# Attention in six TensorE runs a group, and the third gate ahead of the first down, in a perceiver layer

## The chip, the cores and the metric

The kernel runs on one core of one Trainium2 chip. The metric is device time in microseconds of one execution, the median of three runs. Five engines take part: TensorE (PE in the profile; PEld is its weight load), VectorE (DVE), ScalarE (ACT), GpSimd (POOL) and SyncE (SP), which here only issues DMAs. Each engine takes its instructions in the order in which they were emitted.

## The reference

One layer with three stages, all in float32: 16 sequences of 64 tokens of width 1024 attend to a context of 1601 rows each; a gated FFN of inner width 2752 keeps, in each row, only the half of the gate's values that are largest in magnitude; eight rank-16 experts with a top-2 router are added. Cut to what matters:

```python
x = x + xattn(layernorm(x), ctx, ctx, mask)      # 32 heads of 32, 8 KV heads
scores = einsum('bsgrd,btgd->bgrst', xq, xk) / sqrt(32) + mask
probs = softmax(scores)
out = einsum('bgrst,btgd->bsgrd', probs, xv)

s = silu(layernorm(x) @ w_gate.T)
s[the k = 1376 smallest |s| of each row] = 0
x = x + (s * (h @ w_up.T)) @ w_down.T

x = x + experts(layernorm(x))                    # top 2 of 8, rank 16
```

## The kernel before, in words

**Attention.** The work is cut into 64 groups (`Group`, L235): a sequence, one half of the KV heads (4 heads), and half of the query repeats, so that a group has 4 heads with 128 query rows each and 1601 context columns. A group passes through these steps:

- `scores(c)`: for part c of the columns (`PARTS`, L29: 289, 512, 288 and 512 columns), four products, one for each head, each on 32 of TensorE's 128 rows. They go to four PSUM banks: heads 0 to 2 to a bank of their own each (`ps_s`), head 3 to the shared pool `ps_t`.
- `masked(c)`: DVE adds the mask, writes the scores to `sc` in SBUF and takes the maximum over the part; after the last part one small reduction (`nm`) makes the maximum of the row.
- `softmax(g)`: ACT takes the exponential of head g in place, 1601 columns, with its sum.
- `turn(heads)`: TensorE transposes the two heads' 13 blocks of 128 columns. They fill seven tiles of `ps_t`: three of four blocks for each head and one for both last blocks of 65 columns. The tiles are copied to `pT` in SBUF, the first five by ACT, the rest by DVE (one wide copy and two narrow ones).
- `values(c0, c1)`: for blocks c0 to c1, the product of pT with v, each head on 32 of TensorE's columns, summed in the one bank of `ps_o`.
- `keep()`: ACT copies the output of the group to `oT`, DVE takes the reciprocals of the sums.

PSUM has eight banks: `ps_s` three, `ps_o` one, and `ps_t` four (L145). A pool hands its banks out in rotation: the fifth tile gets the bank of the first, and its writer waits until that was read. `ps_t` also holds the query transposes (`turn_queries`) and the transposed outputs (`finish_tile`).

The order is written out by hand in the loop over groups n (L418), in two halves d. In half d TensorE does the long part (512 columns) of the next group's scores, the transposes of heads 2d and 2d+1 of group n, a short part of the scores of group n+1 (d = 0) or n+2 (d = 1), and half of the values of group n-1. That makes eight runs of TensorE in a group. Query transposes of the next tile of tokens stand in the second half of two groups in eight. While attention runs, POOL makes sums and differences of the weights' quarters for the FFN and writes them back to DRAM.

**FFN.** Gate (g), up (u) and down (d) products use seven products of half-size blocks in place of eight, for pairs of token tiles; there are four pairs. Between g and d of a pair, `drop_small` finds each row's threshold: 31 steps, each with one pass of DVE over one tile and one of ACT over the other, then two passes of ranks (`ranks`) to settle ties, and POOL sets the small values to zero. Then TensorE transposes the gated rows (`ptd`), ACT copies them, and the down product follows; then the experts of the pair.

This part is not written out in order. A planner (`Plan`, L1287) simulates the engines when the kernel is built: each step is a task with an engine, an estimated time, its dependencies, a rank and the buffers that it takes, and of the tasks that are ready on an engine, the one with the lowest rank is emitted next. The ranks of the products come from the list `order` (L1235). A task may have a margin: it counts as ready only so long after its dependencies' ends. `normed(..., 15.0)` gives one of 15 us to the normalisation of a pair that is loaded from DRAM.

Of the kernel before, what the change touches and what calls it, by code (L numbers as in the profile page):

```python
# [9 lines left out]
F32 = mybir.dt.float32  # L10
# [10 lines left out]
P = 128  # L21
# [4 lines left out]
NTC = (T + P - 1) // P  # L26
TL = T - (NTC - 1) * P

PARTS = [(0, 289), (289, 801), (801, 1089), (1089, T)]  # L29
NCH = len(PARTS)  # L30
I = 2752
IC = 344
# [22 lines left out]
def tile_perceiver_layer(  # L55
# [78 lines left out]
    a1 = new_pool(early, "a1", 1)  # L134
    ktp = new_pool(early, "kT", 3)
    qtp = new_pool(early, "qT", 2)
    scp = new_pool(early, "sc", 2)
    xnp = new_pool(late, "xn", 1, "right")
    vp = new_pool(late, "v", 3, "right")
    ptp = new_pool(late, "pT", 8, "right")  # L140
    otp = new_pool(late, "oT", 2, "right")
    twp = new_pool(early, "tw", 3)
    xp = new_pool(late, "x", 3, "right")
# [91 lines left out]
    class Group:  # L235


        def __init__(self, b, h, rh):
            self.b, self.h, self.rh = b, h, rh
            self.name = f"{b}_{h}_{rh}"  # L240
            self.sc, self.pT = {}, {}

        def scores(self, c, spare=False):


            b, h, rh = self.b, self.h, self.rh
            if c == 0:
                self.sc = [
                    scp.tile([P, T], F32, tag=f"sc{g}", name=f"sc{g}_{self.name}")
                    for g in range(4)  # L250
                ]
# [4 lines left out]
            t0, t1 = PARTS[c]  # L256
            homes = [[(ps_s, f"ps{g}"), (ps_t, "pt")] for g in range(3)]
            homes.append([(ps_t, "pt"), (ps_o, "po")])
            self.ps = []
            for g in range(4):  # L260
                home, tag = homes[g][spare]
                ps = home.tile([P, 512], F32, tag=tag, name=f"ps{g}_{self.name}_{c}")
                self.ps.append(ps)
            for g in range(4):
                rows = slice(g * HD, (g + 1) * HD)
                q = qT[b // 2][rows, h, b % 2, 2 * rh : 2 * rh + 2, :]
                pe.matmul(
                    self.ps[g][:, : t1 - t0],
                    q.rearrange("p r s -> p (r s)"),
                    kv[b][0][h][rows, t0:t1],  # L270
                    start=True,
                    stop=True,
                )

        def masked(self, c, heads=range(4)):


            t0, t1 = PARTS[c]
            for g in heads:
                dve.tensor_tensor_reduce(  # L280
                    out=self.sc[g][:, t0:t1],
                    in0=self.ps[g][:, : t1 - t0],
                    in1=mask2[:, t0:t1],
                    scale=1.0,
                    scalar=LOWEST,
                    op0=ALU.add,
                    op1=ALU.max,
                    accum_out=self.mx[:, g, c : c + 1],
                )
            if c == NCH - 1 and 2 in heads:  # L290
                self.nm = small.tile([P, 4], F32, tag="nm", name=f"nm_{self.name}")
                dve.tensor_reduce(self.nm, self.mx, AX.X, ALU.max, negate=True)

        def softmax(self, g):

# [108 lines left out]
        pe.transpose(warm[:, 0, :], ident, ident)  # L404
    for h in range(2):
        turn_queries(0, xn, h)
    for group, c in [(groups[0], c) for c in range(NCH)] + [(groups[1], c) for c in range(2)]:
        group.scores(c, spare=c % 2 == 1)
        if c % 2 == 0:
            for _ in range(4):  # L410
                pe.transpose(group.ps[3][:, 3 * P :], ident, ident)
        group.masked(c)
    for g in range(2):
        groups[0].softmax(g)

# [2 lines left out]
    for n in range(ng):  # L418
        i, m = n // 8 + 1, n % 8
        group = groups[n]  # L420
        last = n == ng - 1
        if m == 2 and i < NT:
            load_x(i)
        if m == 4 and n > 8:
            sp_queue.dma_start(xs[i - 2], x[i - 2])
        if n == ng - 3:
            for j in range(2):
                x[j] = xp.tile([P, D], F32, tag="x", name=f"x{j}_f")
                sp_queue.dma_start(x[j], xs[j])
        for d in range(2):  # L430
            add = None
            long = (groups[n + 1], 2 * d + 1) if n + 1 < ng and n + d > 0 else None
            short = (groups[n + 1 + d], 2 - 2 * d) if n + 1 + d < ng else None
            if long:
                long[0].scores(long[1])
            if i < NT and d == 1 and m >= 6:
                turn_queries(i, xn, m - 6)
            if n > 8 and 3 <= 2 * m + d <= 4:
                copy, add = finish_tile(i - 2, 1 - d)
                act.copy(*copy)  # L440
            copies = group.turn((2 * d, 2 * d + 1))
            on_act = 3 if last else 5
            for copy in copies[:on_act]:
                act.copy(*copy)
            if long:
                long[0].masked(long[1], (3, 0, 1, 2))
            for copy in copies[on_act:]:
                dve.tensor_copy(*copy)
            if short:
                short[0].scores(short[1])  # L450
                short[0].masked(short[1])
            if d == 0:
                for g in (2, 3):
                    group.softmax(g)
            elif n + 1 < ng:
                for g in range(2):
                    groups[n + 1].softmax(g)
            if add:
                add()
            if n > 0:  # L460
                groups[n - 1].values(*((0, NTC // 2), (NTC // 2, NTC))[d])
                if d == 1:
                    groups[n - 1].keep()
            if i < NT:
                if (m, d) == (4, 0):
                    norm = Norm(x[i], f"q{i}")
                if (m, d) in ((4, 0), (5, 0)):
                    norm.half(m - 4)
                if (m, d) == (5, 1):
                    norm.end()  # L470
                    xn = scaled_rows(i, norm, pool)
            if d == 1 and 0 <= n - 3 < 3 * NU:
                sums_made(n - 3)
                sums_out(n - 3)
            if d == 1 and 0 <= n - 2 < 3 * NU:
                sums_in(n - 2)
            if last:
                xn = first[d].tile([P, D], F32, tag=("xn", "oT")[d], name=f"xn_f{d}")
                norm = Norm(x[d], f"f{d}")
                norm.half(0)  # L480
                norm.half(1)
                norm.end()
                dve.tensor_scalar(xn, x[d], norm.mean, norm.rstd, ALU.subtract, ALU.mult)
                first_xn[d] = xn
# [232 lines left out]
    def gate(pair, n, rank, after):  # L717
# [10 lines left out]
        for i in pair:  # L728

            def start(i=i):  # L730
                s[i] = sp[i % 6 > 1].tile([P, NIB * P], F32, tag="s", name=f"s{i}")
                pool.memset(s[i][:, I:], 0.0)
                if i not in first_xn:
                    nc.sync.dma_start(s[i][:, D : 2 * D], xs[i])

            t = add("POOL", 0.1, start, after(i), rank)
            if i not in first_xn:
                t = normed(
                    lambda i=i: s[i][:, D : 2 * D], lambda i=i: s[i][:, :D], ahead,
                    f"f{i}", [t], 15.0,  # L740
                )
# [25 lines left out]
    def drop_small(pair, n, gated, after, up):  # L767
# [26 lines left out]
            box["cand"] = cand  # L794
            box["over"] = small.tile([P, 2], F32, tag="over", name=f"over{n}")

        t = add("DVE", 3.4, magnitudes, gated[pair[0]] + gated[pair[1]] + after, 1)
        upped = up([t])
        for bit in range(30, -1, -1):

# [64 lines left out]
        for j, i in enumerate(pair):  # L865
# [32 lines left out]

            t = [t] + [ts1] * j + marked[j]
            for h in range(2):  # L900
                t = [add("DVE", 4.1, lambda h=h, f=ranks: f(h), t, 2)]
            t = add("DVE", 0.6, limits, t + [tb[j]], 2)
            for h in range(2):
                t = add("DVE", 1.75, lambda h=h, f=keep: f(h), [t], 2)
# [327 lines left out]
        return done  # L1232

    pairs = [(i, i + 1) for i in range(0, NT, 2)]
    order = ["g0", "u0", "g1", "d0", "u1", "g2", "g3", "d1", "u2", "d2", "u3", "d3"]  # L1235
    rank = {name: 10 + 10 * j for j, name in enumerate(order)}
    gated = [gate(pairs[0], 0, rank["g0"], lambda i: [])]

# [177 lines left out]
```

## Time and profile before

| what | us |
|---|---|
| three runs | 1723.62, 1723.66, 1723.87 |
| median | 1723.66 |
| the profiled execution | 1721.6 |
| its span, first to last instruction | 1719.8 |

Mean granted TensorE clock: 0.997. By stretches of the span (busy us of each engine):

| stretch, us | PE | DVE | ACT | POOL | DMA share |
|---|---|---|---|---|---|
| 0 to 20: loads, first scores | 16.0 | 12.8 | 3.8 | 7.4 | 0.92 |
| 20 to 836: attention | 814.2 | 687.5 | 757.7 | 310.6 | 0.49 |
| 836 to 1720: FFN, experts | 862.1 | 710.9 | 499.3 | 240.7 | 0.85 |

A row of the timeline has the start in us, the time until the end of the last of its instructions, the engine, the line (L93 is the helper that records every instruction), the operation, the tile written and the tile read, their shapes and how many instructions were merged. In brackets stands idle time of the engine before the row and what ended it. The tiles: `ps` scores, `pt` transposes of the softmax, `po` values, `pg_g` and `pg_u` gate and up, `ptd` transposes before the down, `pd` the down. The ends of matmuls are modelled, so one row can reach into the next; the starts are measured. A float32 matmul leaves two load and two matmul records, a transpose one of each.

### The profile page before, as it was taken

The page shows a single profiled execution, that of the slowest core. Times are in us where ns is not written, and L with a number is a line of the kernel's source. Part 1 is how long each engine was busy: PE and PEld are TensorE (multiplying, and loading weights), DVE is VectorE, ACT ScalarE, POOL GpSimd, SP SyncE. Part 2 cuts the span into 40 slices and gives each one's busy share as a digit, 9 for nine tenths or more (in the row PEclk, how much of TensorE's full clock was granted, in tenths as well). Part 3 has the DMA queues.
Part 4 walks back from the last instruction along what each step waited for, and adds up shares of the span by engine and source line. Part 5 has one row for each costly group of instructions (what it writes and reads, how often), then busy time and mean ns, then how long its engine had stood idle before and what let it go on. Part 6 is the DMA issues. An engine that isn't in the chain of part 4 may idle for free. (4 is left out here: it accounts for less than half of the span.)

```text
span 1719.8 us, 38753 instructions
## 1 busy us (share of the span) xinstructions
PE 1692.3 (98%) x15102; PEld 1151.8 (67%) x15102; DVE 1411.2 (82%) x3655; ACT 1260.8 (73%) x1780; POOL 558.6 (32%) x584
## 2 busy tenths in 40 slices
PE   8999999999999999999999999899999999999999
PEld 6777777777777777777766666446666546645644
DVE  7888888888888888888627999999989999999603
ACT  6999999999999999999544676676737874777010
POOL 2044453454544454110120221512250313332631
PEclk9999999999999999999999999999999999999999
DMA  8236456545556646211599999688989888888873
GB/s 248 85 112 221 144 194 213 186 170 191 172 173 212 204 159 203 70 61 58 193 333 326 307 291 311 210 297 308 301 278 305 266 300 269 285 291 275 317 265 141
DMA packets 132326, 384.56 MB, mean 224 GB/s; under 512 B 9488, under 2 KB 61232, under 8 KB 132144
## 3 DMA queue, kind: packets, MB, share of 16 engines
q1 hardware_dynamic: 113280, 312.83, 55.3%
q0 software_dynamic: 18432, 68.16, 11.7%
q8 instruction: 120, 1.97, 0.5%
q10 hardware_dynamic: 432, 1.09, 0.2%
q14 instruction: 62, 0.51, 0.1%
HBM read 339.58 MB, written 42.47 MB: 222 GB/s over the span
## 5 line engine op out<-in xcount | busy, mean ns | idle before, releaser
L93 DVE CUSTOM_DVE_ANT_0 sc<-ps,mask 128x512 f32<-128x512 f32 (+2 forms) x1024 | 526.3, 571 | 103.1 <-PE ps L93 102.7
L93 ACT ACTIVATE sign<-a,cand 128x2752 int8<-128x2752 f32 x136 | 351.9, 2588 | 107.8 <-DVE cand L93 107.3
L93 ACT ACTIVATE sc<-sc,nm 128x1601 f32<-128x1601 f32 x256 | 420.1, 1666 | 9.6 <-DVE nm L93 9.6
L93 PEld LDWEIGHTS pt<-ident,sc 128*128 128x128 f32 (+1 forms) x3328 | 361.9, 141 | 77.5 <-issue 72.8
L93 PE MATMUL pt<-ident,sc 128*128 128x128 f32 (+1 forms) x3328 | 391.1, 274 | 1.2 <-ACT sc L93 1.1
L93 DVE TENSOR_SCALAR_CACHE_REDUCE junk<-a,cand 128x2752 uint8<-128x2752 f32 x124 | 381.6, 3077 | 3.8
L93 ACT COPY pT<-pt 128x512 f32<-128x512 f32 x636 | 323.8, 607 | 46.2 <-PE pt L93 45.9
L93 PE MATMUL pg_g<-w_g,hS 128*128 128x344 f32 x896 | 263.9, 455 | 6.4 <-DVE s L93 3.3
L93 PE MATMUL pg_u<-w_u,hS 128*128 128x344 f32 x896 | 263.7, 452 | 0.0
L93 POOL TENSOR_TENSOR tw<-tw 128x344 f32<-128x344 f32 (+1 forms) x192 | 176.1, 928 | 267.0 <-DMA tw<-in_wd_dram 89.0
L93 PE MATMUL ps<-kT,qt 32*128 32x512 f32 (+2 forms) x2048 | 247.7, 549 | 3.1 <-DVE mx L93 2.8
L93 PEld LDWEIGHTS pg_g<-w_g,hS 128*128 128x128 f32 x896 | 170.0, 191 | 94.4 <-issue 4.2
L93 PE MATMUL pd<-w_d,s 128*128 128x512 f32 x528 | 231.0, 592 | 0.0
L93 PEld LDWEIGHTS pg_u<-w_u,hS 128*128 128x128 f32 x896 | 168.8, 190 | 86.8 <-issue 3.1
L93 PE MATMUL po<-pT,v 128*32 128x128 f32 x6656 | 208.1, 274 | 0.4 <-ACT oT L93 0.4
L93 PEld LDWEIGHTS po<-pT,v 128*32 128x32 f32 x6656 | 174.1, 110 | 48.6 <-issue 43.7
L93 PEld LDWEIGHTS pd<-w_d,s 128*128 128x128 f32 x528 | 98.6, 190 | 115.3 <-issue 114.8
L93 DVE COPY pT<-pt 65x128 f32<-65x128 f32 (+1 forms) x388 | 141.0, 418 | 23.0 <-PE pt L93 16.0
L93 PEld LDWEIGHTS ps<-kT,qt 32*128 32x128 f32 x2048 | 83.1, 183 | 52.2 <-DVE mx L93 34.8
L93 ACT ACTIVATE s<-s 128x344 f32<-128x344 f32 (+1 forms) x70 | 36.7, 537 | 91.3 <-DVE s L93 90.9
L93 POOL TENSOR_TENSOR s<-s,rank 128x688 f32<-128x688 f32 x32 | 62.4, 1967 | 88.2 <-DVE rank L93 87.4
L93 DVE DVE_READ_ACCUMULATOR2_ANT mx<- 128x1 f32 x1024 | 83.9, 82 | 0.0
(322 smaller groups left out, 1216.5 us busy)
## 6 DMA issues: line engine op xcount, KB each, us to landing
w_g<-ts SPq DMA_DIRECT2D x64, 688.0 KB
w_u<-ts SPq DMA_DIRECT2D x64, 688.0 KB
w_d<-ts SPq DMA_DIRECT2D x48, 768.0 KB
w_g<-in_wg_dram SPq DMA_DIRECT2D x48, 688.0 KB
w_u<-in_wu_dram SPq DMA_DIRECT2D x48, 688.0 KB
w_d<-in_wd_dram SPq DMA_DIRECT2D x36, 768.0 KB
kT<-in_ctx_t_dram SPq DMA_DIRECT2D x31, 800.5 KB
v<-in_ctx_v_dram SPq DMA_DIRECT2D x32, 768.0 KB
```

The lines of the kernel that those rows point to most:

```text
L93: return tc.keep_in_program_order(getattr(self.engine, op)(*args, **kwargs))
```

## The change

**In attention**

- The parts are 512, 512, 512 and 65 columns. The last part is called the rest. Its four products no longer stand in a run with the others: `rests(heads)` makes them for two heads at a time, each into a tile of `ps_t`.
- In half d = 0 of group n, TensorE does part 1 of group n+1, the transposes of heads 0 and 1, the rests of heads 0 and 1 of group n+1 with its part 2, and all values of group n-1. In half d = 1 it does the rests of heads 2 and 3 of group n+1 with part 0 of group n+2, and the transposes of heads 2 and 3. These are six runs.
- The maximum is made for heads 0, 1 and for heads 2, 3 apart (`maxima`). The exponentials of group n+1's heads 0 and 1 are the last of ACT in half 0 and in half 1.
- In half 1 ACT copies four tiles of transposes, DVE two wide and two narrow ones.
- `keep` of group n-1 stands in half 0, ahead of the exponential of head 0. The query transposes stand at the head of half 0.
- Score buffers: two for heads 0, 1, three for heads 2, 3; pT has six buffers for eight. At the start the filler transposes between the scores are gone, and only part 0 of group 1 is made ahead.

**In the FFN's planner**

- The third gate ranks ahead of the first down.
- The margin of a normalisation is 30 for 15; the estimates of `magnitudes` are 4.4 for 3.4 and of `ranks` 4.0 and 5.5 for 4.1.

```diff
-PARTS = [(0, 289), (289, 801), (801, 1089), (1089, T)]
+PARTS = [(0, 512), (512, 1024), (1024, 1536), (1536, T)]
...
-    scp = new_pool(early, "sc", 2)
+    scp = [new_pool(early, "sc", 2), new_pool(early, "sc_late", 3)]
...
-    ptp = new_pool(late, "pT", 8, "right")
+    ptp = new_pool(late, "pT", 6, "right")
...
+        def rests(self, heads):
+            for g in heads:
+                self.rest[g] = ps_t.tile(
+                    [P, 512], F32, tag="pt", name=f"rest{g}_{self.name}"
+                )
+                self.product(g, NCH - 1, self.rest[g])
...
+        def maxima(self, j):
+            if j == 0:
+                self.nm = small.tile([P, 4], F32, tag="nm", name=f"nm_{self.name}")
+            heads = slice(2 * j, 2 * j + 2)
+            dve.tensor_reduce(
+                self.nm[:, heads], self.mx[:, heads], AX.X, ALU.max, negate=True
+            )
...
+        after = groups[n + 1 : n + 3] + [None, None]
         for d in range(2):
             add = None
-            long = (groups[n + 1], 2 * d + 1) if n + 1 < ng and n + d > 0 else None
-            short = (groups[n + 1 + d], 2 - 2 * d) if n + 1 + d < ng else None
-            if long:
-                long[0].scores(long[1])
-            if i < NT and d == 1 and m >= 6:
+            if i < NT and d == 0 and m >= 6:
                 turn_queries(i, xn, m - 6)
+            ahead, c = (after[0], 1) if d == 0 else (after[1], 0)
+            if d == 1 and after[0]:
+                after[0].rests((2, 3))
+            if ahead:
+                ahead.scores(c)
...
             copies = group.turn((2 * d, 2 * d + 1))
-            on_act = 3 if last else 5
+            on_act = 3 if last else 5 - d
             for copy in copies[:on_act]:
                 act.copy(*copy)
-            if long:
-                long[0].masked(long[1], (3, 0, 1, 2))
+            if d == 1 and after[0]:
+                after[0].masked(NCH - 1, (2, 3))
+            if ahead:
+                ahead.masked(c)
+            if d == 1 and after[0]:
+                after[0].maxima(1)
             for copy in copies[on_act:]:
                 dve.tensor_copy(*copy)
-            if short:
-                short[0].scores(short[1])
-                short[0].masked(short[1])
             if d == 0:
                 for g in (2, 3):
                     group.softmax(g)
-            elif n + 1 < ng:
-                for g in range(2):
-                    groups[n + 1].softmax(g)
+                if after[0]:
+                    after[0].rests((0, 1))
+                    after[0].scores(2)
+                    after[0].masked(NCH - 1, (0, 1))
+                    after[0].masked(2, (0, 1))
+                    after[0].maxima(0)
+                    after[0].masked(2, (3, 2))
+                if n > 0:
+                    groups[n - 1].values(0, NTC)
+                    groups[n - 1].keep()
+            if after[0]:
+                after[0].softmax(d)
             if add:
                 add()
-            if n > 0:
-                groups[n - 1].values(*((0, NTC // 2), (NTC // 2, NTC))[d])
-                if d == 1:
-                    groups[n - 1].keep()
...
-                    f"f{i}", [t], 15.0,
+                    f"f{i}", [t], 30.0,
...
-        t = add("DVE", 3.4, magnitudes, gated[pair[0]] + gated[pair[1]] + after, 1)
+        t = add("DVE", 4.4, magnitudes, gated[pair[0]] + gated[pair[1]] + after, 1)
...
-                t = [add("DVE", 4.1, lambda h=h, f=ranks: f(h), t, 2)]
+                t = [add("DVE", 5.5 if j else 4.0, lambda h=h, f=ranks: f(h), t, 2)]
...
-    order = ["g0", "u0", "g1", "d0", "u1", "g2", "g3", "d1", "u2", "d2", "u3", "d3"]
+    order = ["g0", "u0", "g1", "g2", "d0", "u1", "g3", "d1", "u2", "d2", "u3", "d3"]
```

More of the change, by code (lines that the diff above doesn't have):

```diff
@@ L240, in __init__, with product @@
             self.name = f"{b}_{h}_{rh}"
-            self.sc, self.pT = {}, {}
+            self.sc, self.pT, self.rest = {}, {}, {}
+        def rests(self, heads):
[4 more added lines that the diff above has]
+                self.product(g, NCH - 1, self.rest[g])
+        def product(self, g, c, out):
+            b, h, rh = self.b, self.h, self.rh
+            t0, t1 = PARTS[c]
+            rows = slice(g * HD, (g + 1) * HD)
+            q = qT[b // 2][rows, h, b % 2, 2 * rh : 2 * rh + 2, :]
+            pe.matmul(
+                out[:, : t1 - t0],
+                q.rearrange("p r s -> p (r s)"),
+                kv[b][0][h][rows, t0:t1],
+                start=True,
+                stop=True,
+            )
         def scores(self, c, spare=False):
@@ L248, in scores @@
                 self.sc = [
-                    scp.tile([P, T], F32, tag=f"sc{g}", name=f"sc{g}_{self.name}")
+                    scp[g // 2].tile([P, T], F32, tag=f"sc{g}", name=f"sc{g}_{self.name}")
                     for g in range(4)
@@ L255, in scores @@
                     load_kv(b + 1)
-            t0, t1 = PARTS[c]
             homes = [[(ps_s, f"ps{g}"), (ps_t, "pt")] for g in range(3)]
@@ L264, in scores, with masked @@
             for g in range(4):
[L265 to L275, printed above, removed]
+                self.product(g, c, self.ps[g])
+        def masked(self, c, heads=(3, 0, 1, 2)):
             t0, t1 = PARTS[c]
             for g in heads:
+                ps = self.rest[g] if c == NCH - 1 else self.ps[g]
                 dve.tensor_tensor_reduce(
                     out=self.sc[g][:, t0:t1],
-                    in0=self.ps[g][:, : t1 - t0],
+                    in0=ps[:, : t1 - t0],
                     in1=mask2[:, t0:t1],
@@ L289, in masked @@
                 )
-            if c == NCH - 1 and 2 in heads:
+        def maxima(self, j):
+            if j == 0:
                 self.nm = small.tile([P, 4], F32, tag="nm", name=f"nm_{self.name}")
-                dve.tensor_reduce(self.nm, self.mx, AX.X, ALU.max, negate=True)
+            heads = slice(2 * j, 2 * j + 2)
+            dve.tensor_reduce(
+                self.nm[:, heads], self.mx[:, heads], AX.X, ALU.max, negate=True
+            )
         def softmax(self, g):
@@ L406, in tile_perceiver_layer @@
         turn_queries(0, xn, h)
[L407 to L411, printed above, removed]
+    for j, (group, c) in enumerate(
+        [(groups[0], c) for c in range(NCH - 1)] + [(groups[1], 0)]
+    ):
+        if j == 2:
+            group.rests((0, 1))
+        group.scores(c, spare=j % 2 == 1)
+        if j == 2:
+            group.rests((2, 3))
         group.masked(c)
+        if j == 2:
+            group.masked(NCH - 1, range(4))
+            for half in range(2):
+                group.maxima(half)
     for g in range(2):
@@ L466, in tile_perceiver_layer @@
                     norm = Norm(x[i], f"q{i}")
-                if (m, d) in ((4, 0), (5, 0)):
-                    norm.half(m - 4)
-                if (m, d) == (5, 1):
+                if m == 4:
+                    norm.half(d)
+                if (m, d) == (4, 1):
                     norm.end()
+                if (m, d) == (5, 0):
                     xn = scaled_rows(i, norm, pool)
```

## The prediction

> **What bounds the kernel now.** I read the page first. Its engine rows and slices show a TensorE that is never idle for a tenth of a slice, at full clock:
>
> ```profile
> PE 1692.3 (98%) x15102; PEld 1151.8 (67%) x15102; DVE 1411.2 (82%) x3655; ACT 1260.8 (73%) x1780; POOL 558.6 (32%) x584
> ...
> PE   8999999999999999999999999899999999999999
> ...
> PEclk9999999999999999999999999999999999999999
> ```
>
> A busy PE is not yet a bound PE, since its ends are modelled. So I took the timeline of TensorE alone over one group of the attention (starts count, not ends):
>
> ```profile
> 427.51 0.77 PE L93 MATMUL ps<-kT,qt 32*128 32x289 f32 x8
> 428.21 1.74 PE L93 MATMUL po<-pT,v 128*32 128x128 f32 x56
> 429.88 1.14 PE L93 MATMUL ps<-kT,qt 32*128 32x512 f32 x8
> 430.95 3.06 PE L93 MATMUL pt<-ident,sc 128*128 128x128 f32 x26
> 433.94 0.77 PE L93 MATMUL ps<-kT,qt 32*128 32x288 f32 x8
> 434.63 1.52 PE L93 MATMUL po<-pT,v 128*32 128x128 f32 x48
> 436.08 1.14 PE L93 MATMUL ps<-kT,qt 32*128 32x512 f32 x8
> 437.15 3.06 PE L93 MATMUL pt<-ident,sc 128*128 128x128 f32 x26
> 440.14 0.77 PE L93 MATMUL ps<-kT,qt 32*128 32x289 f32 x8
> ```
>
> From start to start: 0.70, 1.67, 1.07, 2.99, 0.69, 1.45, 1.07, 2.99 us, together 12.63 (427.51 to 440.14). Equal runs take equal times, and the waits of TensorE between 100 and 800 us name no engine for more than 0.4 us at a time: the eight runs stand back to back. ACT idles 0.95 us of such a group (0.51 + 0.44, both waiting for transposes). So PE sets the period, and a cost on PE is a cost of the kernel. Fixed costs come from pairs of runs: scores take (1.07 - 0.70)/223 columns = 1.66 ns a column plus 0.22 us a run; values 0.22 us per 8 records plus 0.13 a run.
>
> Next the two other engines beside the transposes that start at 430.95:
>
> ```profile
> 431.70 2.54 ACT L93 COPY pT<-pt 128x512 f32<-128x512 f32 x5 [0.51 <-PE pt L93]
> ```
> ```profile
> 433.83 1.08 DVE L93 COPY pT<-pt 128x512 f32<-128x512 f32 x3
> ```
>
> ACT copies tiles one to five out of PSUM: the first starts 0.75 us after the run's start, the fifth ends at 434.24, 3.29 after it. DVE starts on the sixth at 2.88, as soon as it is there; the groups of instructions by shape give this DVE copy 0.691 us. The run itself lasts 2.99. **The last tiles of a run are copied after the run ends**; today nobody needs their banks then.
>
> In the FFN TensorE is packed too; its timeline has two places with waits, the start of the first down and the fourth gate:
>
> ```profile
> 1079.64 2.74 PE L93 MATMUL pd<-w_d,s 128*128 128x512 f32 x6
> 1084.28 0.93 PE L93 MATMUL ptd<-ident,s 128*128 128x128 f32 x6 [1.90 <-ACT s L93]
> ...
> 1092.74 0.88 PE L93 MATMUL ptd<-ident,s 128*128 128x128 f32 x6 [0.45 <-POOL s L93]
> ...
> 1099.94 1.54 PE L93 MATMUL ptd<-ident,s 128*128 128x128 f32 x6 [2.99 <-ACT s L93]
> ```
> ```profile
> 1258.07 4.32 PE L93 MATMUL pg_g<-w_g,hS 128*128 128x344 f32 x14 [3.26 <-DVE s L93]
> ```
>
> **The change on TensorE, run by run.** A group becomes six runs: scores part 1; transposes of heads 0, 1; two rests (65 columns) with scores part 2; all values; two rests with the next group's part 0; transposes of heads 2, 3.
>
> Removed: one run of scores and one of values, 0.22 + 0.13 = 0.35 us of fixed cost, and 65 columns of the wide runs, 0.11 us: 0.46 a group.
>
> Added: four rest products in two pairs. By columns alone a pair costs 65 x 1.66 ns = 0.11 us. Here a rule speaks against the change. The Trainium skill (TensorE: Matmul & The Clock Gate, LDWEIGHTS) says a weight load costs its columns over 1.2 GHz, whatever the contraction: 128 columns, an estimated 0.107 us. The trace has two loads to a product (2048 load records for the 1024 score products). Under 512 columns the second load hides; under 65 (0.054 us a pass) it doesn't, so a pair costs 2 x 0.107 = 0.21. No row of before has such a narrow product. Bounds: 0.11 by columns, 0.43 if the two row groups don't overlap at all; eight loads in 0.31 us in the trace say that they overlap. I take 0.21.
>
> Without new waits a group would take 12.63 - 0.46 + 0.42 = 12.59: the gain is nearly eaten by the rests, 2 us over 62 groups; with the rests at 0.11 a pair it would be 12.39, and 15 us.
>
> **The new wait.** Transposes, rests and head 3's scores share a pool of four PSUM banks, in rotation. Today seven transposed tiles are followed by one such tile (head 3 of the short part), which gets the bank of tile four, copied 2.73 us into the run (0.75 + 3 x 0.48 + 0.55): no wait. After the change three follow the first run of transposes: rest 0 gets the bank of tile four, rest 1 that of tile five (ACT, 3.29), head 3 of part 2 that of tile six (DVE, 2.88 + 0.69 = 3.57). PE would be there at 2.99. It issues in order, so head 3 starts at 3.57 + 0.05 (a release by DVE at 25.02 was followed by PE at 25.07) = 3.62, 0.63 late, and then the whole 1.07 of a scores run follows. The rests fit inside that wait, so their 0.21 isn't charged here. Run three takes 0.63 + 1.07 = 1.70.
>
> Sum of a group: 1.07 + 2.99 + 1.70 + 2.99 (1.45 + 1.67 - 0.13) + 1.28 (1.07 + 0.21) + 2.99 = **13.02, against 12.63: +0.39**. For 62 groups (the first and last aside) +24 us.
>
> Behind the waiting PE stand all values of the group before; behind those on ACT the oT copy, and behind that, in ACT's order, the exponential of the next group's head 0. It ends at 8.75 + 0.15 + 0.20 + 1.62 = 10.72 after the group's start; the first tile of the second transposes is there at 8.75 + 1.28 + 0.75 = 10.78. That just fits, so I charge nothing; if it is late, ACT's copies are.
>
> Query turns move to the head of a group (14 groups). The extra tile shifts the rotation: head 3 of part 1 then gets the bank of tile five, which DVE now copies, after its four masks and the maxima: 1.29 + 4 x 0.61 + 0.28 + 0.69 = 4.70 after the scores before, where PE is at 1.07 + 2.99 + 0.44 = 4.50. With 0.05: +0.25, x14 = +3 us.
>
> **DVE, ACT and the rest of attention.** Masks stay 16 a group over the same 1601 columns: 12 x 0.61 + 4 x 0.15 equals 8 x 0.61 + 8 x 0.38 within 0.1. DVE gains one copy (0.6) and one maximum (0.28): from 10.7 to 11.6 of 13.0, still covered, but its masks come closer to tile six: up to 0.1 later, which would go onto the wait. ACT loses a copy (0.48); with PE as the bound that is worth nothing. Pools of SBUF (three late score buffers, six pT for eight): the values that free pT now stand earlier on PE than the copies that need it, so nothing. SP's loads and POOL's weight sums keep their places. Start: sixteen filler transposes go and DVE does the same masks; 0, within 1 us.
>
> **FFN.** With the third gate ahead of the first down, the down's transposes and zeroing (POOL 9.8 us for the first tile) are finished behind 66 us of gate work: the waits 1.90 + 0.45 + 2.99 = 5.3 us go. Total products, weights and DMA are the same, and DVE's selection has slack: it ends near 1560, with 155 us of PE work behind it. What is late next is the fourth gate, which needs the first pair's experts, 66 us later now; u1 and d1 stand ready to fill. The 3.26 us wait comes from DVE's ranks (4.19 us scans) ahead of PSUM sums; the longer planner times should place them better, but the ranks now fall under u1's sums: I take half, 1.6. FFN: -7, bounds -10 (both go, and the 1.4 us holes before expert turns) and +2.
>
> **Sum.** 24 + 3 - 7 = +20. On the profiled execution, 1721.6 us (span 1719.8): 1741.6; the median stands 2.1 above it, 1723.66, so **1743.7 us**.
>
> **Rivals.**
> A, the forecast, 0.66: 1734 to 1754.
> B, the other side, 0.15: the wait for tiles five and six is not there (the pool gives another bank, or the copies end inside the run), and rests cost 0.11 a pair: 12.63 - 0.46 + 0.22 = 12.39, -15 us, and FFN -7: 1702. For it: two switches really go. Against: four banks and 2.88 + 0.69 leave no room. It decides where tile six is free by 2.99; the break-even with FFN's 7 us is a group at +0.11, a wait below about 0.3.
> C, 0.13: a second engine follows. DVE's masks make tile six late and ACT's exponential, queued behind the oT copy, delays the next transposes: 0.1 + 0.2 more a group, +19: about 1762.
> D, 0.06: rests under the scores are free (-0.21) and FFN gains 10: +11 + 3 - 10 = about 1728.
>
> **How the numbers follow.** Two tenths of a per cent, 3.4 us, is about what a measurement of this kernel can tell from no change. B is faster (0.15), D's low end and gaps between cases give same 0.04, the rest slower 0.81. The range 1718 to 1762 holds A and D, half of C, and leaves B out.
>
> **What would show it.** In the changed kernel's TensorE timeline: six runs a group; the run of 65- and 512-column scores after transposes of heads 0, 1 starting with a wait on ACT pT and DVE pT of 0.3 to 0.7 us; 13.0 us between groups; 2.99 us for the 104 value records; the first down without its 5.3 us. Wrong would be: groups of 12.4 to 12.6 with no wait at the rests (B), idle ACT gone (C), or the FFN not shorter.

## The result, and the profile after

| | us |
|---|---|
| before, median of 4 runs beside the change | 1723.64 (1723.26 to 1723.87) |
| after, median of 4 runs | 1755.6 (1751.79 to 1756.05) |
| ratio, with its 95% interval | 1.0184 (1.0172 to 1.0197) |
| predicted | 1743.7, range 1718 to 1762 |
| the profiled execution of after, and its span | 1755.33 and 1753.5 |

The change costs 32 us. The page of after shows as full a TensorE as before, with 30 us more of "busy" time for fewer instructions:

```profile
PE 1722.0 (98%) x15090; PEld 1186.3 (68%) x15090; DVE 1460.6 (83%) x3782; ACT 1237.2 (71%) x1717; POOL 559.1 (32%) x584
...
PE   8999999999999999999999999999989999999999
...
PEclk8999999999999999999999999999999999999999
```

Short waits are covered by the modelled ends of the matmuls and count as busy, so the page can't tell where the time went. The starts can. TensorE's timeline of after over a plain group (one without query transposes), where the brackets with idle time are absent although TensorE waits:

```profile
451.77 3.06 PE L93 MATMUL pt<-ident,sc 128*128 128x128 f32 x26
454.75 0.68 PE L93 MATMUL rest<-kT,qt 32*128 32x65 f32 x3
455.12 0.70 PE L93 MATMUL ps<-kT,qt 32*128 32x512 f32 x2
455.27 0.27 PE L93 MATMUL rest<-kT,qt 32*128 32x65 f32 x1
455.38 1.13 PE L93 MATMUL ps<-kT,qt 32*128 32x512 f32 x6
456.44 3.05 PE L93 MATMUL po<-pT,v 128*32 128x128 f32 x104
459.42 0.33 PE L93 MATMUL rest<-kT,qt 32*128 32x65 f32 x2
459.43 0.70 PE L93 MATMUL ps<-kT,qt 32*128 32x512 f32 x2
459.58 0.28 PE L93 MATMUL rest<-kT,qt 32*128 32x65 f32 x2
459.69 1.08 PE L93 MATMUL ps<-kT,qt 32*128 32x512 f32 x6
460.70 3.06 PE L93 MATMUL pt<-ident,sc 128*128 128x128 f32 x26
463.69 1.14 PE L93 MATMUL ps<-kT,qt 32*128 32x512 f32 x8
464.76 1.42 PE L93 MATMUL pt<-ident,sc 128*128 128x128 f32 x11
```

From start to start: 2.98, 1.69 (rests and part 2), 2.98, 1.28 (rests and part 0), 2.99, 1.07; a group takes 12.99 us (451.77 to 464.76). Two runs with products of the same shapes differ by 0.41 us: the one at 459.42 is free, the one at 454.75 waits. In the free run the last six wide records start 0.27 after the first rest, in the other 0.63 after it. The timelines of ACT and then DVE at the same moment show for what:

```profile
452.51 2.54 ACT L93 COPY pT<-pt 128x512 f32<-128x512 f32 x5 [0.39 <-PE pt L93]
```
```profile
454.64 1.08 DVE L93 COPY pT<-pt 128x512 f32<-128x512 f32 x3
```

ACT's fifth copy ends at 455.05, and then rest 1 can start in the bank of tile five (the third rest record stands at 455.11). The first of DVE's three copies lasts 0.69 us and reads tile six. It ends at 455.33, and at 455.38 TensorE writes head 3's scores into that bank. Tile six is the wait that ends last.

By stretches of the two profiled executions (starts of the first transposes of a group; 33.7 us in all):

| stretch | before | after | difference |
|---|---|---|---|
| start of the span to group 2 | 45.73 | 51.95 | +6.2 |
| group 2 to group 63 (61 groups) | 781.60 | 810.35 | +28.8 |
| group 63 to the first gate product | 18.03 | 17.26 | -0.8 |
| first gate to the last product | 870.1 | 869.5 | -0.6 |

So the attention's groups lose nearly all of it, the start some, and the FFN gives next to nothing back in this execution.

### The profile page after: what moved, and what is told of

Read it like the earlier page. It is cut to its first block, busy times and chain, and to the rows that moved or that the text cites. A ratio compares the mean times of both kernels' runs of the same rounds, so it can differ in the third digit from the quotient of the medians.

```text
span 1753.5 us, 38510 instructions
## 1 busy us (share of the span) xinstructions
PE 1722.0 (98%) x15090; PEld 1186.3 (68%) x15090; DVE 1460.6 (83%) x3782; ACT 1237.2 (71%) x1717; POOL 559.1 (32%) x584
## 4 chain that ended last, share of the span: by engine, by line
PE 72%; DVE 18%; issue 4%; POOL 2%; ACT 2%; DMA 1%; SPq 0%; DVEq 0%; ACTq 0%; POOLq 0%
PE pt L93 20%; PE ps L93 11%; PE po L93 11%; PE pg_u L93 10%; DVE junk L93 10%; PE pd L93 9%; PE pg_g L93 5%; PE rest L93 3%; POOL s L93 2%; DVE sc L93 1%; DVE s L93 1%; DVE rank L93 1%; ACT sign L93 1%; DVE pT L93 1%; DVE cand L93 1%
## 5 line engine op out<-in xcount | busy, mean ns | idle before, releaser
L93 DVE CUSTOM_DVE_ANT_0 sc<-ps,mask 128x512 f32<-128x512 f32 x768 | 488.8, 687 | 65.2 <-PE ps L93 62.3
L93 ACT ACTIVATE sc<-sc,nm 128x1601 f32<-128x1601 f32 x256 | 421.2, 1657 | 11.3 <-DVE nm L93 11.3
L93 PE MATMUL pt<-ident,sc 128*128 128x128 f32 (+1 forms) x3328 | 395.4, 276 | 3.9 <-DVE mx L93 3.5
L93 ACT COPY pT<-pt 128x512 f32<-128x512 f32 x573 | 293.8, 605 | 31.5 <-PE pt L93 31.1
L93 PE MATMUL ps<-kT,qt 32*128 32x512 f32 x1536 | 254.0, 642 | 1.9 <-DVE mx L93 1.7
L93 PEld LDWEIGHTS po<-pT,v 128*32 128x32 f32 x6656 | 177.9, 110 | 47.4 <-issue 47.4
L93 PE MATMUL po<-pT,v 128*32 128x128 f32 x6656 | 195.1, 274 | 0.0
L93 DVE COPY pT<-pt 65x128 f32<-65x128 f32 (+1 forms) x451 | 178.1, 453 | 17.0 <-PE pt L93 10.8
L93 PEld LDWEIGHTS ps<-kT,qt 32*128 32x128 f32 x1536 | 92.4, 186 | 15.1 <-issue 9.1
```

Source lines behind the costliest of these rows:

```text
L93: return tc.keep_in_program_order(getattr(self.engine, op)(*args, **kwargs))
```

## The experiments

### Which half of the change carries the loss

`attn_only` is after with the FFN's planner as before, `ffn_only` is before with the FFN's four edits:

```diff
-                    f"f{i}", [t], 15.0,
+                    f"f{i}", [t], 30.0,
...
-        t = add("DVE", 3.4, magnitudes, gated[pair[0]] + gated[pair[1]] + after, 1)
+        t = add("DVE", 4.4, magnitudes, gated[pair[0]] + gated[pair[1]] + after, 1)
...
-                t = [add("DVE", 4.1, lambda h=h, f=ranks: f(h), t, 2)]
+                t = [add("DVE", 5.5 if j else 4.0, lambda h=h, f=ranks: f(h), t, 2)]
...
-    order = ["g0", "u0", "g1", "d0", "u1", "g2", "g3", "d1", "u2", "d2", "u3", "d3"]
+    order = ["g0", "u0", "g1", "g2", "d0", "u1", "g3", "d1", "u2", "d2", "u3", "d3"]
```

> The changed kernel with the FFN's planner as before. Theory: all of the loss is attention's, 34 us up to the first gate: 1755.6 + 0.6 = about 1756 us, first gate at 879.6 us of the span as in the changed kernel. Rival: the FFN's edits are worth 7 us beside this attention: about 1762 us.

> The kernel before with the four edits of the FFN's planner alone. Theory: in the changed kernel the FFN took 869.5 us from the first gate to the last matmul against 870.1 before, because the waits that go at the first down (5.3 us) and in the fourth gate (3.3 us) come back at the start of the second down, where TensorE has no gate left to fill with. That has nothing to do with attention, so this kernel takes 1723.6 - 0.6 = about 1723 us, with waits of 5 to 10 us between the second up and the second down. Rival (the term of the prediction): the FFN gains 7 us by itself and lost them to something that attention brought: about 1717 us, without those waits.

`attn_only` took 1754.27 us (ratio 1.0178, 1.0157 to 1.0200): within its interval the whole loss. `ffn_only` took 1721.19 (ratio 0.9986, 0.9978 to 0.9994): 2.6 us gained, between the theory (0.6) and its rival (7). The waits at the second down that after shows (below) are in `ffn_only` too, 2.62 and 2.13 us, so the attention doesn't cause them.

### The wait for the banks

`no_first_rests` makes no rest products of heads 0 and 1 in half 0. The masks of their last 65 columns read 65 columns of part 2, so DVE does the same work. The pool then has one tile behind the transposes, and head 3 gets the bank of tile four.

```diff
-                    after[0].rests((0, 1))
                     after[0].scores(2)
-                    after[0].masked(NCH - 1, (0, 1))
+                    after[0].masked(NCH - 1, (0, 1), after[0].ps)
```

> The changed kernel without the two rest products of heads 0 and 1 in the first half of a group; DVE masks the first 65 columns of part 2 in their place, so their last 65 scores are not the reference's. Theory (bank wait): without these two tiles head 3 of part 2 gets the bank of the fourth transposed tile, free before the run ends, so the run takes 1.07 us in place of 1.69 and a plain group 12.99 - 0.62 = 12.37 us. Rival (the products themselves cost, by their weight loads and the narrow columns, 0.1 to 0.2 us, and the rest of the 0.62 is not the bank's): 12.78 to 12.9 us.

`late_copies` does the opposite: DVE, in place of ACT, copies tile five of the first transposes too, ahead of tile six.

```diff
-            on_act = 3 if last else 5 - d
+            on_act = 3 if last else 4
```

> The changed kernel with four of the first half's transposed tiles copied by ACT in place of five; DVE copies the fifth and sixth, so that the sixth is free at about 4.05 us after the transposes' start in place of 3.57. Theory (bank wait): head 3 of part 2 starts 0.48 us later, a plain group takes 12.99 + 0.48 = 13.47 us. Rival (the wait is not for the copies): 12.99 us, as ACT and DVE have time to spare.

TensorE's timelines of the two, first without the first rests, then with the late copies, over the same part of a plain group:

```profile
432.39 3.06 PE L93 MATMUL pt<-ident,sc 128*128 128x128 f32 x26
435.38 1.14 PE L93 MATMUL ps<-kT,qt 32*128 32x512 f32 x8
436.45 3.05 PE L93 MATMUL po<-pT,v 128*32 128x128 f32 x104
```
```profile
453.50 0.74 PE L93 MATMUL rest<-kT,qt 32*128 32x65 f32 x3
...
454.19 1.44 PE L93 MATMUL ps<-kT,qt 32*128 32x512 f32 x6
455.56 3.05 PE L93 MATMUL po<-pT,v 128*32 128x128 f32 x104
```

Without the rests the run takes 1.07 (435.38 to 436.45), a group 12.38, and the kernel 1713.45 us in one run. The 0.61 that a group loses here is the wait and the products together: two rests cost 0.21 where nothing waits (1.28 against 1.07), and 0.41 is the wait beyond that. With a later tile six the run grows to 2.06 (453.50 to 455.56), a group to 13.37 and the kernel to 1776.07 in one run. The growth is 0.38, not the 0.48 expected: DVE, which waits 0.13 us for tile six in after, goes here from its masks straight on to tile five (453.18). Its copy of tile six ends at 454.46 and head 3 starts at 454.51, 4.00 after the transposes' start against 3.61 in after. The bank of tile six, and the engine that empties it, set the group.

### The same six runs without the wait

`rests_a_group_early` keeps the six runs, the parts and all 65-column products. All four rests stand in half 1 beside part 0 of the same group, heads 0 to 2 ahead of it in the pool of the transposes and head 3 behind it in the bank of `ps_o`, so that no rest follows the first transposes. At the start group 0's rests stand behind its part 2, and the statistics of the query tile are spread over two groups.

```diff
+                home, tag = (ps_o, "po") if g == 3 else (ps_t, "pt")
...
-            if d == 1 and after[0]:
-                after[0].rests((2, 3))
+            if d == 1 and ahead:
+                ahead.rests((0, 1, 2))
             if ahead:
                 ahead.scores(c)
+            if d == 1 and ahead:
+                ahead.rests((3,))
...
-                    after[0].rests((0, 1))
                     after[0].scores(2)
-                    after[0].masked(NCH - 1, (0, 1))
```

> The two repairs, and all four rest products made a group earlier, in the second half beside part 0 of the same group: heads 0 to 2 ahead of it in the shared pool, head 3 behind it in the bank of the values. One tile of the pool follows the first transposes, as in the kernel before. Theory (bank wait): run three takes 1.07 us, the run with part 0 keeps its 1.28 as four row groups load beside each other, so TensorE's runs add up to 1.07 + 2.99 + 1.07 + 2.98 + 1.28 + 2.99 = 12.38 us a group, 0.25 below the kernel before: about 1707 us, below both kernels. Rival: six runs cost in another way (DVE or ACT fall behind, or four rests in one run cost 0.43), then a group takes 12.6 us or more and the time is 1722 us or more.

It took 1714.81 us against 1722.64 (ratio 0.9949, 0.9929 to 0.9968). Its TensorE over a group:

```profile
431.17 3.06 PE L93 MATMUL pt<-ident,sc 128*128 128x128 f32 x26
434.15 1.14 PE L93 MATMUL ps<-kT,qt 32*128 32x512 f32 x8
435.22 3.05 PE L93 MATMUL po<-pT,v 128*32 128x128 f32 x104
438.20 0.33 PE L93 MATMUL rest<-kT,qt 32*128 32x65 f32 x3
...
439.49 3.06 PE L93 MATMUL pt<-ident,sc 128*128 128x128 f32 x26
```

Four rests and part 0 take 1.29 (438.20 to 439.49), against 1.28 for two rests and part 0 in after: the four row groups work side by side, and a run of rests costs 0.21 to 0.22 whether it has two or four. The group is at 12.38, 0.25 below before. This closes the sum: 12.63 - 0.46 (two switches and 65 wide columns) + 0.21 = 12.38; after has a second pair of rests and the wait, about 0.21 + 0.41, and so 12.99. The total came out 8 us above the 1707 expected: the start stayed slow (second group at 38.52 us) and the sixth group of each eight kept a wait of 0.40.

### The start, and the sixth group of eight

TensorE's timeline of the start of after, and its busy time and granted clock by windows (the columns are the window, its length, busy us of PE, PEld, DVE, ACT and POOL with their instructions, PE's clock, DMA share and GB/s); the last two lines are those windows of before:

```profile
13.79 0.48 PE L93 MATMUL rest<-kT,qt 32*128 32x65 f32 x2 [3.95 <-DMA kT<-in_ctx_t_dram]
...
32.65 5.30 PE L93 MATMUL pt<-ident,sc 128*128 128x128 f32 x26
```
```profile
20.00:24.00 4.00, 4.00 (x22) 2.13 (x15) 2.45 (x9) 2.96 (x4) 0.00 (x0) 0.54 1.01 372
...
34.00:40.00 6.00, 6.00 (x39) 5.07 (x39) 3.88 (x14) 4.11 (x7) 0.00 (x0) 0.72 0.16 37
```
```profile
20.00:24.00 4.00, 3.66 (x30) 3.02 (x34) 2.88 (x9) 4.00 (x9) 0.00 (x0) 1.00 1.05 336
...
34.00:40.00 6.00, 6.00 (x90) 4.49 (x89) 4.85 (x18) 5.56 (x10) 0.18 (x1) 1.00 0.71 238
```

Rests 0 and 1 of the first group stand ahead of part 2 and need the last columns of kT, so everything behind them waits 3.95 us for the last transfer. From 14 to 20 us the granted clock is 0.50. It comes back to 1.00 from 24 to 28 and falls again after 28: the transposes from 32.65 to 37.88 run at 0.56 and take 5.23 us where they take 2.99 elsewhere. Before has 1.00 in all windows from 20 to 40 us.

In the sixth group of each eight (n = 5) the two views of after, TensorE and then DVE, are these:

```profile
90.93 1.53 PE L93 MATMUL pt<-ident,sc 128*128 128x128 f32 x12
92.96 1.72 PE L93 MATMUL pt<-ident,sc 128*128 128x128 f32 x14 [0.50 <-DVE mx L93]
```
```profile
89.51 1.67 DVE L93 COPY pT<-pt 128x512 f32<-128x512 f32 x4
91.10 0.68 DVE L93 BATCH_NORM_STATS2 st_q<-x 128x6 f32<-128x512 f32 x1
...
92.12 0.68 DVE L93 CUSTOM_DVE_ANT_0 sc<-ps,mask 128x512 f32<-128x512 f32 x1
```

The second half of the next query tile's statistics stands in DVE's queue between the copies and the mask of head 3. Head 3's bank stays full until that mask has read it at 92.8, and a transposed tile waits for it. The change itself put the statistics there, though the list of the change doesn't name it:

```diff
-                if (m, d) in ((4, 0), (5, 0)):
-                    norm.half(m - 4)
-                if (m, d) == (5, 1):
+                if m == 4:
+                    norm.half(d)
+                if (m, d) == (4, 1):
                     norm.end()
```

`start_and_norm` puts the first group's rests behind its part 2 and that half of the statistics back into the next group:

```diff
-        if j == 2:
-            group.rests((0, 1))
         group.scores(c, spare=j % 2 == 1)
         if j == 2:
-            group.rests((2, 3))
+            group.rests(range(4))
...
-                if m == 4:
-                    norm.half(d)
-                if (m, d) == (4, 1):
+                if (m, d) in ((4, 0), (5, 0)):
+                    norm.half(m - 4)
+                if (m, d) == (5, 0):
                     norm.end()
```

> The changed kernel with two repairs. At the start the four rest products stand behind part 2, in place of two ahead of it; the second half of a query tile's statistics and their end stand in the first half of the next group. Theory: the groups of 14.26 us (a wait of 0.5 us for DVE within the transposes) go to about 13.5, 7 times 0.7 = 5 us; and the start, which waited 3.95 us for the last piece of kT, gets 2 to 3 us faster: 1755.6 - 7.5 = about 1748 us. Rivals: for the start, that the missing filler transposes and the lower clock cost the 6 us, then it stays 6 us late, 1751 us; for the long groups, that it is the query transposes themselves, then they stay at 14.26.

1747.21 us, ratio 1.0144 (1.0126 to 1.0162). The long groups take 13.51 for 14.26, seven times, as expected. The second group starts at 34.30 for 38.96, more than the 2 to 3 us expected.

Not all of that is the edit. `rests_a_group_early` also has the first group's rests behind part 2, but all four rests of group 1 there as well, ahead of the first transposes; its second group came at 38.52. `early_filled` adds to that kernel 32 transposes of the identity between the scores of the start, to keep TensorE occupied:

```diff
+        if j > 0:
+            fill = ps_t.tile([P, 4, P], F32, tag="pt", name=f"fill{j}")
+            for _ in range((0, 12, 8, 12)[j]):
+                pe.transpose(fill[:, 0, :], ident, ident)
```

> The kernel with the rests a group early, and 32 filler transposes between the scores of the start. Theory: the start is late because TensorE, idle between the pieces, is granted half its clock (0.50 to 0.60 between 14 and 24 us); with fillers the clock stays up, the second group's transposes start at 35 us or earlier in place of 38.5, and the time is 1711 us. Rival: the start is set by the arrival of kT and DVE's masks: 38.5 us again, 1715 us.

1716.58 us (ratio 0.9966, 0.9955 to 0.9977) against 0.9949 for the kernel without them: no gain is shown. What happens in the start shows only when kernels with the same start are put side by side, one profile each:

| start as in | profile | second group, us | clock 30 to 34, 34 to 38, 38 to 42 us |
|---|---|---|---|
| after | after | 38.96 | 0.56, 0.59, 1.00 |
| | `attn_only` | 39.45 | 0.63, 0.52, 1.00 |
| | `margin_15` | 36.32 | 1.00, 1.00, 1.00 |
| `start_and_norm` | `start_and_norm` | 34.30 | 1.00, 1.00, 1.00 |
| `rests_a_group_early` | `rests_a_group_early` | 38.52 | 0.79, 0.79, 1.00 |
| `early_filled` | `early_filled` | 43.29 | 1.00, 0.62, 0.53 |
| | `early_filled_costs` | 37.41 | 1.00, 1.00, 1.00 |

The same start differs by 3.1 us and by 5.9 us between profiles, and each time the late one is the one whose clock fell a second time. At full clock the start of after costs 3.2 us against before (36.32 and 33.10), and moving the two rests behind part 2 takes back 2.0 of it (34.30). The other 2.6 of the 5.9 us in after go with the clock; the slowed transposes alone are 2.2 of them. What decides whether it falls again, and whether the fillers help against it, one profile each can't show.

### The FFN: order, times or margin

The waits of TensorE in the FFN of after, summed by what was waited for (us in total, times, longest):

```profile
PE ptd L93 <- ACT s L93: 3.8, 4, 2.1
PE pt_f L93 <- ACT s L93: 2.6, 1, 2.6
...
PE pt_m L93 <- DVE xd L93: 2.1, 1, 2.1
```

The 3.26 us of the fourth gate (a wait for DVE) and the waits at the first down are gone; none of these rows is theirs. Others have come at the second down. TensorE there in after, then POOL's queue just before, then ACT's:

```profile
1292.07 0.60 PE L93 MATMUL ptd<-ident,s 128*128 128x128 f32 x4
1295.28 0.66 PE L93 MATMUL pt_f<-ident,s 128*128 128x128 f32 x4 [2.61 <-ACT s L93]
1298.06 1.11 PE L93 MATMUL ptd<-ident,s 128*128 128x128 f32 x4 [2.13 <-ACT s L93]
1298.97 5.07 PE L93 MATMUL pd<-w_d,s 128*128 128x512 f32 x6
...
1304.75 2.74 PE L93 MATMUL pd<-w_d,s 128*128 128x512 f32 x6
```
```profile
1285.62 3.56 POOL L93 TENSOR_TENSOR s<-s,rank 128x688 f32<-128x688 f32 x2
1289.15 3.63 POOL L93 TENSOR_TENSOR s<-s,v_u_(2, 0)_16352 128x344 f32<-128x344 f32 x1
1292.86 0.19 POOL L93 TENSOR_SCALAR ve_f<-sq_f 128x1 f32<-128x1 f32 x1
```
```profile
1293.98 1.24 ACT L93 ACTIVATE s<-s,shift_f,rstd_f 128x1024 f32<-128x1024 f32 x1 [12.78 <-POOL shift_f L93]
...
1297.44 0.56 ACT L93 COPY s<-ptd 128x512 f32<-128x512 f32 x1
```

The second up ends, and both waits are for ACT. The first one is the fourth gate's: it needs a normalisation. ACT has its squares by 1280.1, but the small step that follows (`ve_f`) stands in POOL's queue, behind zeroing and products of the up, until 1292.86, and ACT stands idle for 12.78 us until POOL's `shift_f`. The second one is the down's: its first transposes were written at 1292.07, so their zeroing was done, but the copy that empties their bank stands in ACT's queue behind the normalisation, until 1297.44. After the two waits six down products take 4.90 us (1298.97 to 1303.87) where six later take 2.57; the granted clock between 1298 and 1304 was 0.53.

Three runs ask which of the edits did this. `margin_15` is after with the margin alone back at 15, `costs_only` is before with margin and times but the order as it was, and `early_filled_costs` is `early_filled` with only the order put back.

> The changed kernel with the margin of a normalisation back at 15 us. Theory: the waits at the second down come because the fourth gate, the only work that could fill there, is put off: it needs the first pair's experts, which stand 66 us later, and then the planner waits 30 us more for its load. With 15 us its transposes come about 15 us earlier, TensorE has gate work while ACT copies the second down's transposes, and 5 us of the waits go: about 1750 us. Rival: the gate is late by the experts alone, or ACT is the one that is late: within 1 us of the changed kernel, 1755 us.

> The kernel before with the longer planner times and the margin alone, the order of products as before. Theory: the order is what moves the waits from the first down to the second; with the order as before the first down keeps its 5.3 us or a part of them, the second down has gate work to fill and none, and the longer times for the ranks take away the 3.3 us in the fourth gate: 1720 us, 2 to 4 below the kernel before. Rival: the longer times are what makes the second down late, then its waits of 5 us and more are here too and the time is 1724 us or more.

> The same, with the order of the FFN's products as before and the longer planner times. Theory: attention and FFN are apart, so this differs from the run with the changed order by what costs_only differs from ffn_only, -1 us or so: 1710 us. Rival: the order is worth more beside this attention, then it is slower by 2 us and more.

`margin_15` stayed at 1756.25 (1.0195, 1.0179 to 1.0212). Its waits at the second down are other ones, 1.60 us in place of 2.61 and 2.13, and a new one of 4.99 some nine us later: the margin moves the waits and doesn't remove them. `costs_only` took 1716.51 (0.9956, 0.9941 to 0.9970): longer times and margin together bring about 7 us, where they bring 2.6 with the new order. `early_filled_costs` took 1712.35 (0.9935, 0.9912 to 0.9958), 4 us below `early_filled`. In both pairs the new order takes 4 to 5 us away by the medians, though the intervals of the second pair just touch, and the profiles of that pair differ by 5.9 us in the start.

The FFN alone, from the first gate to the last product, tells the edits apart better. In one profile each, with the time in which TensorE's row is not busy:

| kernel | order | times | margin | FFN, us | TensorE idle in it, us |
|---|---|---|---|---|---|
| before | old | old | 15 | 870.1 | 16.3 |
| `attn_only` | old | old | 15 | 869.9 | 16.3 |
| `costs_only` | old | longer | 30 | 865.5 | 11.6 |
| `early_filled_costs` | old | longer | 30 | 863.1 | 11.3 |
| `ffn_only` | new | longer | 30 | 868.7 | 13.1 |
| after | new | longer | 30 | 869.5 | 13.9 |
| `early_filled` | new | longer | 30 | 865.8 | 13.2 |
| `margin_15` | new | longer | 15 | 871.7 | 15.7 |

The idle time hardly depends on the attention. Times and margin together take 4.7 us of it away, the new order gives about 2 back, and with the new order the margin of 30 is worth about 2; the longer times alone were not run. In `costs_only` the first down still waits 5.2 us, as before, but the fourth gate waits 0.5 for 3.26. The FFN itself also varies by 3.7 us among the three kernels with all four edits, so the -0.6 of the table of stretches is one execution of several; the busy part, 852.6 to 855.6 us for the same products, goes with the clock (last section).

### The parts together

`early_best` has the early rests, the FFN's order of before with the longer times and the margin, group 1's rests behind the first transposes for the start, and the statistics of the query tile earlier by a group. Cut to what differs from `rests_a_group_early`:

```diff
+                    if n == 0:
+                        after[0].rests(range(4))
                     after[0].scores(2)
+                    if n == 0:
+                        after[0].masked(NCH - 1, range(4))
...
-                if (m, d) in ((4, 0), (5, 0)):
-                    norm.half(m - 4)
+                if (m, d) in ((3, 0), (4, 0)):
+                    norm.half(m - 3)
...
-    order = ["g0", "u0", "g1", "g2", "d0", "u1", "g3", "d1", "u2", "d2", "u3", "d3"]
+    order = ["g0", "u0", "g1", "d0", "u1", "g2", "g3", "d1", "u2", "d2", "u3", "d3"]
```

> All four rest products a group early, the FFN in the order of before with the longer planner times, no added transposes; the four rests of group 1 stand in group 0's first half behind its transposes instead of at the start; the statistics of the query tiles a turn each, (3,0), (4,0) and (5,0). Theory: the parts add up. The run with the early rests was 1714.8 with its plain group at 12.38 and its third-gate order; taking the order of before with longer times is worth about 5 us (1721.2 to 1716.5 on the kernel before); the groups of query tiles lose their 0.40 us wait for the masks, 7 x 0.4 = 3 us; the second group starts near 34 instead of 38.5, about 4 us: 1714.8 - 5 - 3 - 4 = about 1703, between 1700 and 1708. Rival: the start is set by the arrival of kT's last piece and by a low granted clock, wherever the rests stand, and the second group stays at 37 to 39: about 1707 to 1712.

1706.12 us against 1723.47, ratio 0.9900 (0.9883 to 0.9916), in the range of the theory and 3 us above its centre. The second group starts at 34.30, the groups of query tiles take 12.90, the FFN from first gate to last product 866.9. The six runs that cost 1.8% in after are part of a kernel that is 1.0% faster than before, of which the FFN's times and margin brought 0.4% by themselves in `costs_only`.

## Why the prediction came out as it did

- **TensorE as the bound, and the sum of a group: right.** 13.02 was predicted and 12.99 measured, term by term: 1.70 against 1.69, 2.99 against 2.98, 1.28 against 1.28. The copy of tile six was put at 2.88 after the run's start and head 3 at 3.62; they came at 2.87 and 3.61. That this wait, and not something beside it, is the loss was shown by taking it away with its products (12.38), by lengthening it (13.37), and by keeping all four products where nothing waits (12.38).
- **The rest products: the size is right.** 0.21 a run stands between the 0.11 by columns and the 0.43 for row groups one after another. The two load records of one rest start 0.11 us apart in after (454.75 and 454.86), as the rule on weight loads of the Trainium skill (TensorE: Matmul & The Clock Gate, LDWEIGHTS) has it, and two of them make the 0.21. That the load is what costs is not shown apart: no run changed it alone.
- **Groups around the query tiles: too small a term.** +0.25 in 14 groups was charged, 3.5 us. Measured against plain groups, the two long groups of eight had 0.88 more before (2 x 0.44) and have 1.79 in after (1.27 + 0.52); the difference of 0.91 times seven is 6.4 us. Of it, 0.75 is the statistics on DVE in the sixth group, which the change had moved there and the sum had not looked at: `start_and_norm` took that out. What is left is 0.08 a group (0.52 against 0.44), so the wait that was charged, tile five behind four masks and the maxima, is mostly not there.
- **The start: the term failed.** "0, within 1 us" became +6.2. The sum counted the operations removed and didn't ask on which transfer the two rests ahead of part 2 depend, nor what idle time does to the clock there. By the second group the loss is 5.9 us: 2.0 by the place of the two rests, 2.6 that go with a clock that fell again in after and `attn_only` and not in `margin_15`, and 1.2 that were not followed up.
- **FFN: the step that failed.** -7 was charged, and the profile has -0.6, the medians of `ffn_only` -2.6. The waits named did go. The fourth gate was rightly named as late next, but "u1 and d1 stand ready to fill" was wrong: u1 ends too early, the fourth gate's normalisation waits for POOL, and d1's transposes for a copy behind that normalisation on ACT. The new order only moves the place without filler from the first down to the second, and costs about 2 us of idle time. The gain that there is comes from the longer times with the margin, which were credited with 1.6 us and take away 4.7 us of idle time without the new order.
- **The rivals.** B's group of 12.39 is real, but only where no rest follows the first transposes; its claim that the wait isn't there was false for this kernel. C's mechanism, DVE late with its masks, appears in the sixth group alone; in a plain group DVE is there for tile six as forecast (2.87). Its time of 1762 was nearer to the result than the forecast, for another reason. D's free rests are not there: the pair that doesn't wait costs 0.21.

The direction and the largest term were right. The result lies in the range, but above the forecast's own 1734 to 1754. The miss of 13.7 us on the profiled execution is 6 of start, 6 of FFN and 2 of groups, where the plain groups, charged 2 us too high (24 against 61 times 0.36, 22), hide part of what the groups around the query tiles cost beyond their term.

## What to carry to other kernels

With a rotating pool of PSUM banks, write down for each tile which earlier tile held its bank and when that is read. A small product moved behind a full run of tiles can wait longer than it lasts, and the same product costs little a few runs away (0.22 us for four here). In a kernel whose engines start idle, ask of each product made earlier which transfer it needs; and before an order fills one hole, check that the filler isn't queued behind the same engine.

## What the hardware showed beyond expectation

- **The clock falls after short waits, and not by the same amount each time.** After two waits of 2.61 and 2.13 us with 0.66 of work between them the granted clock was 0.53 in after, and the next six products took 2.3 us longer than the 2.57 of six later ones: the waits cost half as much again as their length. The same two waits stand in `early_filled` and `ffn_only`, where the six products took 3.56 and 5.10 us. So two profiles with equal waits can differ by 1.5 us at one place. The Trainium skill (TensorE: Matmul & The Clock Gate, What's actually happening) puts the fall to half rate after about 3.4 us of idle time and calls the phase variable from run to run. The rows fit this if the little work between the two waits doesn't count as busy, which no run here tests.
- **POOL beside a scan of DVE.** In after a product of 128x344 on POOL took 0.91 us at 1293.90 and 3.63 twice beside DVE's scan of ranks (1282.03 and 1289.15), ending both times 0.71 us after the scan:

```profile
1280.76 4.19 DVE L93 TENSOR_TENSOR_SCAN rank<-junk 128x1376 int16<-128x1376 uint8 x1
...
1287.88 4.19 DVE L93 TENSOR_TENSOR_SCAN rank<-junk 128x1376 int16<-128x1376 uint8 x1
```

The scans end at 1284.95 and 1292.07, POOL's products at 1285.66 and 1292.78. The planner prices such a product at 0.9. The Trainium skill (SBUF — State Buffer, SBUF: two separate sides) describes a port pair shared by the two engines as a lock held for a whole instruction, which is what these ends look like; no run here took the scan away.
